# Rounding steps and normalisations written as two-input instructions, and zeros filled elsewhere, in a four-layer sequence kernel

## The chip, the cores and the metric

The kernel runs on one core of one Trainium2 chip. The metric is the device time of one execution in microseconds. Everything is computed in fp32. The engines are TensorE (PE; PEld is its loading of weights), VectorE (DVE), ScalarE (ACT) and GpSimd (POOL); SyncE (SP) issues the DMAs.

## What is computed

The input x has 16 sequences (B) of 512 tokens (T) with 256 channels (C). Four layers run one after the other, each with its input added and a layer normalisation behind it, `(v - mean) / sqrt(var + 1e-5)`:

- attention with 16 heads, causal, whose queries and keys are projected into latents of 32 values and rotated by position;
- a feed-forward layer 256 -> 704 -> 256, `down(silu(gate) * up)`, in which the inputs and weights of the products are first rounded to FP4;
- a recurrence over the 512 tokens with a tanh of its states;
- a channel mix, `sigmoid(xr Wr) * (relu(xk Wk)^2 Wv)`, where xr and xk blend each token with the one before it.

The rounding to FP4 is what the change is about. Each row is cut into blocks of 16 values:

```python
def fp4_quant_dequant(x):
    xb = x.reshape(shape[:-1] + (shape[-1] // BLOCK, BLOCK))
    scale = jnp.max(jnp.abs(xb), axis=-1, keepdims=True) / 6.0
    scale = jnp.maximum(scale, jnp.float32(1e-12))
    xn = xb / scale
    idx = jnp.searchsorted(_MID, jnp.abs(xn))
    q = _GRID[idx] * jnp.sign(xn) * scale
    return q.reshape(shape)
```

## The kernel before

**Stage 1** (about 0 to 1765 us of the profiled execution) runs attention and the feed-forward layer together. A loop (from L788) goes over slots (b, g, n): 16 sequences, 4 groups of heads, 3 pieces of the causal triangle. Each slot computes scores (`S`, L524), masks them and takes their maximum on DVE (L536), takes exponentials on ACT (L549), turns the result on PE (L559; ACT copies it out, L561) and weights the values with it (L590; `vpad` holds the values with zeros between the heads). Beside each half slot the loop places steps of other work by a hand-written plan: latents (PE L457, DVE L467 and L472), values, heads, the output projection of a finished sequence (L482 to L506), and for 128 tokens at a time `quantize`, `ffn_up` (L281 on) and `ffn_down`. The order of PE's instructions is fixed by this program text. The orders of the other engines come from a scheduler, which places instructions by their estimated times.

PE's results go to seven PSUM banks in rotation. A group of matmuls takes the bank used seven groups before and waits until the engine that reads that bank has done so. Two such readers matter below: L304 and L307 in `ffn_up` (DVE, the gate and the product with `up`) and L536.

**The rounding** is `fp4`, L181 to L215, a generator whose `yield`s let the plan spread its instructions: it goes on a list, of which `vector_step` takes one step at a time, and `vector_done` all that a consumer still needs. The DVE part takes the maximum of the block (L201), its scale (L202), the reciprocal (L203), a correction by one unit of the last place (L204), the scaled values (L207), the power of two of each (L209, L210), and adds a constant that rounds (L213). POOL then takes the constant away (L214) and multiplies by the scale (L215). Inputs to `ffn_up` have 256 columns (16 blocks), inputs to `ffn_down` 704 (44 blocks). Their tiles `q_sc`, `q_inv`, `q_q` and `q_m` have two buffers each.

**The normalisations.** The statistics come from DVE (L91, L92), `rstd_of` (L81 to L87) takes the power -0.5 on POOL, and one DVE instruction subtracts the mean and multiplies: L502 behind the attention, L98 in `layernorm` behind the feed-forward layer, L891 in `normalized` in the second half of the kernel.

**Between the stages** (about 1765 to 1860 us) the last output projection is followed by the rounding and the feed-forward layer of the last 512 tokens, in an order given by the list `FIRST` (L1092). `N` in it is `normed`, the first step of the recurrence: DVE L859, POOL L863 to L867, then PE L883. In the same stretch POOL fills `hist`, the buffers of the recurrence's states, with zeros (L1008).

**Stage 2** (from about 1860 us) steps through the 512 tokens (L1167 on): `advance_state` multiplies a state (PE L1060) and takes its tanh on ACT into `hist` (L1068), twice per token, with the other steps of the layers beside it.

At the start of stage 1 DVE copies two columns (`cabk`, L394), while POOL fills `vpad` with zeros (L400). `values` (L415) writes the heads between these zeros later.

Of the kernel before, what the change touches and what calls it, by code (L numbers as in the profile page):

```python
# [10 lines left out]
F32 = mybir.dt.float32  # L11
# [3 lines left out]
AF = mybir.ActivationFunctionType  # L15
ALU = mybir.AluOpType
# [3 lines left out]
P = 128  # L20
B, T, C = 16, 512, 256
# [38 lines left out]
def tile_kernel(ctx: ExitStack, tc: tile.TileContext, I: dict, out: bass.AP):  # L60
    nc = tc.nc


    const = ctx.enter_context(tc.tile_pool(name="const", bufs=1))
# [3 lines left out]
    make_identity(nc, ident)  # L68
    neg_half = const.tile([P, 4], F32, name="neg_half")
    nc.gpsimd.memset(neg_half, -0.5)  # L70
    cols = const.tile([P, NCOLS], F32, name="cols")
    nc.sync.dma_start(cols, I["cols"])

# [7 lines left out]
    def rstd_of(mv, n, eps):  # L81

        ve = small.tile([P, 4], F32, tag="ve", name="ve")
        nc.gpsimd.tensor_scalar(ve[:, :n], mv[:, :n, 1], 1.0, eps, ALU.mult, ALU.add)  # L84
        rs = small.tile([P, 4], F32, tag="rstd", name="rstd")
        nc.gpsimd.tensor_tensor(rs[:, :n], ve[:, :n], neg_half[:, :n], ALU.pow)
        return rs  # L87

    def stats_into(mv_slice, x):
        st = small.tile([P, 6], F32, tag="bnst", name="bnst")  # L90
        nc.vector.bn_stats(st, x)  # L91
        nc.vector.bn_aggr(mv_slice, st)  # L92

    def layernorm(dst, src):
        mv = small.tile([P, 4, 2], F32, tag="mv", name="mv")
        stats_into(mv[:, 0, :], src)
        rs = rstd_of(mv, 1, LN_EPS)
        nc.vector.tensor_scalar(dst, src, mv[:, 0, 0:1], rs[:, 0:1], ALU.subtract, ALU.mult)  # L98

# [3 lines left out]
    def recurrent_weights():  # L105

        ta = own.tile([P, 2, 4, P], F32, name="ta")  # L110
        wb = own.tile([P, 4, 2, 2, P], F32, name="wb")
        nc.gpsimd.memset(wb, 0.0)
        wc = own.tile([P, 4, 2, 32], F32, name="wc")
        nc.gpsimd.memset(wc, 0.0)
        for par, quarters in enumerate(QUARTERS):
            for i, (r, c) in enumerate(quarters):

                e = i % 2
                of, rs, cs = slice(e * 64, e * 64 + 64), slice(r * 64, r * 64 + 64), slice(c * 64, c * 64 + 64)
                nc.sync.dma_start(ta[rs, par, :, cs], I["bda"][of, i // 2 :: 2, of])  # L120
                if par == 0:
                    nc.sync.dma_start(
                        wc[cs, :, r, c * 16 : c * 16 + 16],
                        I["bdc"][of, i // 2 :: 2, e * 16 : e * 16 + 16],
                    )
                for q2 in range(2):
                    at = slice(q2 * 64 + i * 16, q2 * 64 + i * 16 + 16)
                    nc.sync.dma_start(
                        wb[at, q2::2, par, r, cs], I["bdb"][at, q2 * 2 + i // 2 :: 4, of]
                    )  # L130
        nc.scalar.activation(ta, ta, AF.Tanh)
        for k in ("woutT", "wrT", "wkT", "wvT"):
            sq[k] = own.tile([P, 2, C], F32, name=k)
            nc.sync.dma_start(sq[k], I[k].rearrange("(n p) c -> p n c", p=P))
        bout = own.tile([P, C], F32, name="bout")
        nc.sync.dma_start(bout, I["bout"].to_broadcast([P, C]))
        nc.vector.tensor_scalar(bout, bout, 0.5, None, ALU.mult)
        return ta, wb, wc, bout
# [9 lines left out]
    def mm(name):  # L148
        banks.append(banks.pop(0))
        return banks[-1].tile([P, 512], F32, tag="mm", name=name)  # L150
# [30 lines left out]
    def fp4(dst, x, nb, rows=P):  # L181

        n = nb * 16
        sc = ffn.tile([P, 44], F32, tag="q_sc", name="q_sc", bufs=2)[:rows, :nb]  # L190
        inv = ffn.tile([P, 44], F32, tag="q_inv", name="q_inv", bufs=2)[:rows, :nb]
        q = ffn.tile([P, FF], F32, tag="q_q", name="q_q", bufs=2)[:rows, :n]
        m = ffn.tile([P, FF], F32, tag="q_m", name="q_m", bufs=2)[:rows, :n]

        def blocks(t):
            return t.rearrange("p (n k) -> p n k", k=16)

        def over(t):
            return t.unsqueeze(2).to_broadcast([rows, nb, 16])

        nc.vector.tensor_reduce(sc, blocks(x), AX.X, ALU.max, apply_absolute_value=True)  # L201
        nc.vector.tensor_scalar(sc, sc, 1.0 / 6.0, 1e-12, ALU.mult, ALU.max)  # L202
        nc.vector.reciprocal(inv, sc)  # L203
        nc.vector.tensor_scalar(inv, inv, 1.0 - 2.0**-23, None, ALU.mult)  # L204
        if n > C:
            yield
        nc.vector.tensor_tensor(blocks(q), blocks(x), over(inv), ALU.mult)  # L207
        yield
        nc.vector.tensor_scalar(m.bitcast(U32), q.bitcast(U32), 0x7F800000, None, ALU.bitwise_and)  # L209
        nc.vector.tensor_scalar(m, m, 1.0, 1.5 * 2.0**22, ALU.max, ALU.mult)  # L210
        if n > C:
            yield
        nc.vector.tensor_tensor(q, q, m, ALU.add)  # L213
        nc.gpsimd.tensor_tensor(q, q, m, ALU.subtract)  # L214
        nc.gpsimd.tensor_tensor(blocks(dst), blocks(q), over(sc), ALU.mult)  # L215
# [56 lines left out]
    def quantize(b, j):  # L272
        xq_of[b, j] = xq = ffn.tile([P, C], F32, tag="xq", name="xq", bufs=2)
        queue(("x", b, j), fp4(xq, x_of[b][:, j, :], C // 16))
        yield 0.0
# [65 lines left out]
    with ExitStack() as a:  # L341
# [54 lines left out]
            )  # L396

        vpad = [wts.tile([P, NT, H, 32], F32, name=f"vpad{i}") for i in range(2)]
        for i in range(2):
            nc.gpsimd.memset(vpad[i], 0.0)  # L400

# [78 lines left out]
        def out_projection(b):  # L482
            while b not in whole:
                yield None
            x, yT = x_of[b], y_of.pop(b)
            for j in range(0, NT, 2):
                mv = small.tile([P, 4, 2], F32, tag="mv", name="mv")
                ps = mm("ps_o")
                for i in range(2):
                    for hf in range(2):  # L490
                        nc.tensor.matmul(
                            ps[:, i * C : i * C + C],
                            yT[:, hf, (j + i) * P : (j + i) * P + P], cpT[:, hf, :],
                            start=hf == 0, stop=hf == 1,
                        )
                both = x[:, j : j + 2, :].rearrange("p j c -> p (j c)")
                nc.vector.tensor_tensor(both, ps, both, ALU.add)
                for i in range(2):
                    stats_into(mv[:, i, :], x[:, j + i, :])
                rs = rstd_of(mv, 2, LN_EPS)  # L500
                for i in range(2):
                    nc.vector.tensor_scalar(  # L502
                        x[:, j + i, :], x[:, j + i, :], mv[:, i, 0:1], rs[:, i : i + 1],
                        ALU.subtract, ALU.mult,
                    )
                yield 0.9  # L506

# [108 lines left out]
        def pause(b):  # L616
# [9 lines left out]

        TASKS = {
            "L": latents, "H": heads, "V": values, "O": out_projection, "Q": quantize,
            "U": lambda b, j: whole_steps(ffn_up(b, j)), "D": lambda b, j: whole_steps(ffn_down(b, j)),
            "W": lambda b: ffn_weights(), "P": pause,  # L630
# [67 lines left out]
        with tc.manual_schedule(engines={mybir.EngineType.PE}), ExitStack() as s:  # L698
# [8 lines left out]
            rows = prep.tile([1, C], F32, name="rows")  # L707
# [74 lines left out]
        ps_b = five.enter_context(tc.tile_pool(name="ps_b", bufs=5, space=PSUM))  # L782
        ps_y = five.enter_context(tc.tile_pool(name="ps_y", bufs=1, space=PSUM))
        banks[:] = [ps_2] * 2 + [ps_b] * 5

        with tc.manual_schedule(engines={mybir.EngineType.PE}):
            slots = [(b, g, n) for b in range(B) for g in range(4) for n in range(len(BLOCKS))]
# [3 lines left out]
            for slot in slots + [None]:  # L791
                if slot:
                    b, g, n = slot
                    if g == 0 and n == 0:
# [5 lines left out]
                        if b == 2:  # L800
                            ta, wb, wc, bout = recurrent_weights()
# [20 lines left out]
                before = (slot, ps) if slot else None  # L822
            divide()
            last_projection = out_projection(B - 1)
            next(last_projection)
            quantize_now(0)
# [151 lines left out]
    def value(p):  # L978
# [24 lines left out]
    hist = [  # L1003
        [wts.tile([P, 8, 2, 64], F32, name=f"hist{g}{i}") for i in range(2)] for g in range(2)
    ]
    for g in range(2):
        for i in range(2):
            nc.gpsimd.memset(hist[g][i], 0.0)  # L1008
    state = [None, None]
    clean, ot_of = {}, {}  # L1010

# [113 lines left out]
    with tc.manual_schedule(engines={mybir.EngineType.PE}):  # L1125
# [41 lines left out]
        for t in range(T):  # L1167
# [9 lines left out]
            for g in range(2):  # L1177
                if us[g] is None or us[g][0] + us[g][1] == t:
                    t0, n = starts[g].pop(0)
# [6 lines left out]
            if t % 8 == 7:  # L1186
                at = t % 16 - 7
                for g in range(2):
                    old, new = hist[g][t // 8 % 2], clean[t // 16, g]
                    old = old.rearrange("p t k (r s b) -> p t k r s b", r=2, s=2)  # L1190
                    for r in range(2):
                        rs, qs = slice(r * 64, r * 64 + 64), slice(64 - r * 64, 128 - r * 64)
# [108 lines left out]
```

## Time and profile before

| | |
|---|---|
| median of 3 runs | 2583.96 us (2583.03 to 2585.3) |
| profiled execution | 2582.77 us |
| its span, from the first to the last instruction | 2581.0 us |
| mean granted clock of TensorE, as a share of the full | 0.983 |
| instructions in the span | 73861 |

The busy time of the engines in 40 equal slices of the span, in tenths (9 is 90% or more), with the granted clock of TensorE:

```profile
PE   8789999999999999999999999996899999999997
DVE  6767888787887888878888788887566666666665
ACT  4656666666666666666666666753366666666663
POOL 4322333333333333333333333333555555555653
PEclk9899999999999999999999999998899999999999
```

The slice is 64.5 us wide. From the third slice to the 27th the picture hardly changes: that is stage 1. The drop of PE behind it is the stretch between the stages, and the last third is the recurrence. PE is close to full throughout; DVE is the next, at some 80% in stage 1.

The groups of instructions by line give the busy time of a group, the mean time of one instruction in nanoseconds, and after the second bar the idle time of the engine just before it. Those of the rounding's small steps on DVE, separate by form:

```profile
L204 DVE TENSOR_SCALAR q_inv<-q_inv 128x16 f32<-128x16 f32 x74 | 31.2, 424 | 1.0
L202 DVE TENSOR_SCALAR q_sc<-q_sc 128x44 f32<-128x44 f32 x66 | 28.5, 432 | 1.1
L204 DVE TENSOR_SCALAR q_inv<-q_inv 128x44 f32<-128x44 f32 x66 | 23.6, 357 | 1.1
L202 DVE TENSOR_SCALAR q_sc<-q_sc 128x16 f32<-128x16 f32 x74 | 17.9, 253 | 0.2
```

Such a mean can stand far from the usual duration of the instruction, so the views of single lines, with minimum, median and maximum, are read beside it:

```profile
L204 DVE TENSOR_SCALAR q_inv<-q_inv x142: 138/176/1595, 15.5 to 1834.0; 128x16 f32<-128x16 f32 x74, 128x44 f32<-128x44 f32 x66, 64x16 f32<-64x16 f32 x2
L202 DVE TENSOR_SCALAR q_sc<-q_sc x142: 110/186/1470, 14.4 to 1831.8; 128x16 f32<-128x16 f32 x74, 128x44 f32<-128x44 f32 x66, 64x16 f32<-64x16 f32 x2
```

In the timeline, a row is a run of equal instructions on one engine: start and duration in microseconds, what is computed from what, how many, and in square brackets how long the engine had been idle and what ended that. In the view of waits, a row names the waiting engine and line, what it waited for, the total, the number of waits and the longest.

### The profile page before, as it was taken

Reading aid. Unit: us, or ns where it says so; the run is one execution under the profiler, and the core shown is the slowest. Engines: PE = TensorE matmul, PEld = TensorE weight load, DVE = VectorE, ACT = ScalarE, POOL = GpSimd, SP = SyncE. Lnnn points to the kernel's source line nnn. Section 1 sums busy time; section 2 is a strip of 40 time slices with the busy share of each in tenths; the row PEclk is TensorE's granted clock in tenths of the full one; section 3 lists DMA queues with packets and bytes.
Section 4 is the critical chain, followed back from the end, with each engine's and each line's share of the span. In section 5 each row is a group of like instructions: output and inputs, shape, how many; then the busy total and the mean of one; then the engine's idle time right before and its main releaser. Section 6 shows DMA issues by size and latency. Waiting matters only on the chain.

```text
span 2581.0 us, 73861 instructions
## 1 busy us (share of the span) xinstructions
PE 2438.0 (94%) x28802; PEld 1715.8 (66%) x28802; DVE 1946.9 (75%) x5621; ACT 1615.6 (63%) x5532; POOL 1048.2 (41%) x1649
## 2 busy tenths in 40 slices
PE   8789999999999999999999999996899999999997
PEld 4456666666666666666666666664677777777775
DVE  6767888787887888878888788887566666666665
ACT  4656666666666666666666666753366666666663
POOL 4322333333333333333333333333555555555653
PEclk9899999999999999999999999998899999999999
DMA  3000000000000000000000000000101111111100
GB/s 118 22 10 5 22 13 16 13 15 16 19 14 16 15 12 23 14 16 15 12 24 14 15 15 4 15 14 9 49 29 40 37 38 40 40 38 37 35 28 22
DMA packets 58016, 61.30 MB, mean 24 GB/s; under 512 B 7873, under 2 KB 53058, under 8 KB 57666
## 3 DMA queue, kind: packets, MB, share of 16 engines
q1 hardware_dynamic: 56802, 55.54, 6.9%
q8 instruction: 226, 3.70, 0.6%
q10 hardware_dynamic: 864, 1.05, 0.1%
q14 instruction: 124, 1.02, 0.1%
HBM read 39.79 MB, written 16.78 MB: 22 GB/s over the span
## 4 chain that ended last, share of the span: by engine, by line
PE 58%; DVE 27%; ACT 7%; POOL 4%; issue 3%; DMA 0%; ACTq 0%; POOLq 0%; DVEq 0%; SPq 0%
PE u L1060 7%; PE ps_pt L559 6%; PE S L524 5%; DVE p L536 5%; PE u L1020 4%; PE pg L160 4%; PE pu L160 3%; PE py L590 3%; ACT p L549 3%; PE ps_h L439 3%; PE ps_d L160 2%; PE ps_a L904 2%; PE ps_k L904 2%; ACT pT L561 2%; PE ps_q L457 2%
## 5 line engine op out<-in xcount | busy, mean ns | idle before, releaser
L549 ACT ACTIVATE p<-p,nm 128x512 f32<-128x512 f32 (+3 forms) x1024 | 569.7, 561 | 520.8 <-DVE nm L536 516.7
L1068 ACT ACTIVATE hist<-u 64x64 f32<-64x64 f32 x2048 | 447.3, 218 | 250.8 <-PE u L1060 182.5
L536 DVE CUSTOM_DVE_ANT_0 p<-S,mask 128x512 f32<-128x512 f32 (+3 forms) x1024 | 443.7, 483 | 50.1 <-PE S L524 50.1
L559 PEld LDWEIGHTS ps_pt<-ident,p 128*128 128x128 f32 x2560 | 296.7, 141 | 235.5 <-issue 86.2
L1060 PEld LDWEIGHTS u<-hist,ta 128*64 128x64 f32 x8176 | 362.9, 138 | 121.0 <-ACT hist L1068 41.6
L559 PE MATMUL ps_pt<-ident,p 128*128 128x128 f32 x2560 | 393.6, 280 | 9.2 <-DVE nm L536 3.5
L561 ACT COPY pT<-ps_pt 128x384 f32<-128x384 f32 (+1 forms) x768 | 370.3, 515 | 38.9 <-PE ps_pt L559 38.6
L1060 PE MATMUL u<-hist,ta 128*64 128x32 f32 x8176 | 384.2, 219 | 4.8 <-ACT hist L1068 4.5
L214 POOL TENSOR_TENSOR q_q<-q_q,q_m 128x256 f32<-128x256 f32 (+1 forms) x142 | 168.7, 1188 | 457.0 <-DVE q_q L213 442.7
L524 PE MATMUL S<-kc,qr 32*128 32x128 f32 (+3 forms) x2048 | 235.7, 474 | 8.9 <-ACT qr L478 7.9
L1020 PE MATMUL u<-xt,wb 128*64 128x64 f32 x4128 | 223.2, 230 | 3.5 <-issue 2.4
L549 ACT ACTIVATION_READ_ACCUMULATOR p<-p,nm 128x1 f32 x1024 | 198.9, 194 | 0.0
L160 PE MATMUL pg<-wgT,xqT 128*128 128x352 f32 x512 | 177.5, 470 | 4.2 <-ACT xqT L289 2.9
L473 POOL TENSOR_TENSOR qc<-qc,qs 128x512 f32<-128x512 f32 x64 | 81.6, 1275 | 236.0 <-DVE qs L472 230.9
L160 PE MATMUL pu<-wuT,xqT 128*128 128x352 f32 x512 | 172.5, 459 | 1.2 <-DVE th L304 1.2
L160 PE MATMUL ps_d<-wdT,hT 128*128 128x256 f32 x732 | 169.5, 381 | 2.2 <-ACT hT L323 2.2
L1020 PEld LDWEIGHTS u<-xt,wb 128*64 128x64 f32 x4128 | 165.0, 139 | 9.4 <-issue 3.0
L590 PEld LDWEIGHTS py<-pT,vpad 128*32 128x32 f32 x5120 | 141.2, 110 | 43.2 <-issue 30.7
L590 PE MATMUL py<-pT,vpad 128*32 128x128 f32 x5120 | 165.3, 276 | 3.8 <-ACT pT L561 3.5
L524 PEld LDWEIGHTS S<-kc,qr 32*128 32x128 f32 x2048 | 111.0, 185 | 78.2 <-issue 32.0
L160 PEld LDWEIGHTS ps_d<-wdT,hT 128*128 128x128 f32 x732 | 134.8, 191 | 19.6 <-ACT hT L323 3.1
L84 POOL TENSOR_SCALAR ve<-mv 128x1 f32<-128x1 f32 (+1 forms) x160 | 32.8, 205 | 264.5 <-DVE mv L92 234.7
(164 smaller groups left out, 4620.4 us busy)
## 6 DMA issues: line engine op xcount, KB each, us to landing
xT<-in_xT_dram SPq DMA_DIRECT2D x16, 512.0 KB
x<-in_x_dram SPq DMA_DIRECT2D x16, 512.0 KB
xs<-x SPq DMA_DIRECT2D x64, 128.0 KB
x<-xs SPq DMA_DIRECT2D x32, 256.0 KB
xm<-xs SPq DMA_DIRECT2D x32, 256.0 KB
out_dram<-o SPq DMA_DIRECT2D x64, 128.0 KB
w<-in_w_down_dram SPq DMA_DIRECT2D x2, 352.0 KB
w<-in_w_gate_dram SPq DMA_DIRECT2D x5, 128.0 KB
```

Of the source, the lines that this page charges most:

```text
L160: nc.tensor.matmul(dst, left, right, start=start, stop=stop)
L214: nc.gpsimd.tensor_tensor(q, q, m, ALU.subtract)
L524: nc.tensor.matmul(S[h][:, at : at + w], q[rs, i * P : i * P + P], k[rs, :w], start=True, stop=True,)
L536: nc.vector.tensor_tensor_reduce(out=p[:, own], in0=S[h][:, own], in1=mask[:, T - (i + 1) * P :], scale=1.0, scalar=-MASKED, op0=ALU.add, ...
L549: nc.scalar.activation(p[:, own], p[:, own], AF.Exp, bias=nm[:, u : u + 1], scale=-1.0, accum_out=sum_of[b, g][:, cb, half, h : h + 1],)
L559: nc.tensor.transpose(ps[:, at : at + P], p[:, at : at + P], ident)
L561: nc.scalar.copy(pT[:, :w], ps[:, :w])
L590: nc.tensor.matmul(py[q * 32 : q * 32 + 32, PLACE[i][1], :], vpad[b % 2][:, j, g * 4 + h, :], pt, start=j == 0 and h % 2 == 0, stop=j == i ...
L904: nc.tensor.matmul(dst[cs], left[:, cs], right, start=first, stop=not first)
L1020: nc.tensor.matmul(u[rs, k, par:n:2, bs : bs + 16], wb[:, g * 2 + k, par, half, rs], xt[:, g, at : at + n - par : 2, :], start=par == 0 an ...
L1060: nc.tensor.matmul(into[cs, :, c, :], ta[:, t % 2, g * 2 + k, cs], own[:, :, c, :], start=False, stop=True, skip_group_check=True,)
L1068: nc.scalar.activation(state[g][rs, :, r * 32 : r * 32 + 32].rearrange("p k (s b) -> p k s b", s=2), u[rs, :, t - t0, :] .rearrange("p k ( ...
```

## The change

It has four parts.

1. In `fp4` the correction of L204 is no longer an instruction of its own. L207 becomes a SCALAR_TENSOR_TENSOR that multiplies by the constant and by the reciprocal; L202 becomes one too, which takes its lower bound from a small tile `tiny` filled at the start.
2. The normalisations of L98 and L502 change from TENSOR_SCALAR to SCALAR_TENSOR_TENSOR, with the reciprocal deviation spread over the columns as second input. L891 is not changed.
3. The zeros of `vpad` are filled by the same POOL instructions, but written behind the preparation, just ahead of the loop of stage 1.
4. The zeros of `hist` are made by ACT, as the product of another tile (`ta`, weights of the recurrence) with 0, instead of by POOL.

```diff
+    tiny = const.tile([P, 44], F32, name="tiny")
+    nc.gpsimd.memset(tiny, 1e-12)
...
-        nc.vector.tensor_scalar(dst, src, mv[:, 0, 0:1], rs[:, 0:1], ALU.subtract, ALU.mult)
+        nc.vector.scalar_tensor_tensor(
+            dst, src, mv[:, 0, 0:1], rs[:, 0:1].to_broadcast([P, C]), ALU.subtract, ALU.mult
+        )
...
-        nc.vector.tensor_scalar(sc, sc, 1.0 / 6.0, 1e-12, ALU.mult, ALU.max)
+        nc.vector.scalar_tensor_tensor(sc, sc, 1.0 / 6.0, tiny[:rows, :nb], ALU.mult, ALU.max)
         nc.vector.reciprocal(inv, sc)
-        nc.vector.tensor_scalar(inv, inv, 1.0 - 2.0**-23, None, ALU.mult)
         if n > C:
             yield
-        nc.vector.tensor_tensor(blocks(q), blocks(x), over(inv), ALU.mult)
+        nc.vector.scalar_tensor_tensor(
+            blocks(q), blocks(x), 1.0 - 2.0**-23, over(inv), ALU.mult, ALU.mult
+        )
...
         vpad = [wts.tile([P, NT, H, 32], F32, name=f"vpad{i}") for i in range(2)]
-        for i in range(2):
-            nc.gpsimd.memset(vpad[i], 0.0)
...
-                    nc.vector.tensor_scalar(
-                        x[:, j + i, :], x[:, j + i, :], mv[:, i, 0:1], rs[:, i : i + 1],
-                        ALU.subtract, ALU.mult,
+                    nc.vector.scalar_tensor_tensor(
+                        x[:, j + i, :], x[:, j + i, :], mv[:, i, 0:1],
+                        rs[:, i : i + 1].to_broadcast([P, C]), ALU.subtract, ALU.mult,
                     )
...
         banks[:] = [ps_2] * 2 + [ps_b] * 5
+        for i in range(2):
+            nc.gpsimd.memset(vpad[i], 0.0)
...
-            nc.gpsimd.memset(hist[g][i], 0.0)
+            nc.scalar.activation(
+                hist[g][i].rearrange("p t k n -> p (t k n)"), ta.rearrange("p a k n -> p (a k n)"),
+                AF.Identity, scale=0.0,
+            )
```

Line numbers here and below are those of the kernel before, unless another kernel is named.

## Prediction, made before the changed kernel ran

> **What bounds the kernel now.** I read the totals first, then the stage in which nearly all of the rounding runs, then that stage's waits, and last single stretches of its timeline.
>
> ```profile
> PE 2438.0 (94%) x28802; PEld 1715.8 (66%) x28802; DVE 1946.9 (75%) x5621; ACT 1615.6 (63%) x5532; POOL 1048.2 (41%) x1649
> PE 58%; DVE 27%; ACT 7%; POOL 4%; issue 3%; DMA 0%; ACTq 0%; POOLq 0%; DVEq 0%; SPq 0%
> ```
>
> TensorE is busy 94% of the span, yet VectorE, the only engine on which this change removes work, holds 27% of the chain of waits. So DVE time counts only where TensorE waits for it. Stage 1 repeats every 108 us, once per batch, and b = 2 to 14 are 13 such blocks with the same pattern. One block, in the busy times per stretch (PE, PEld, DVE, ACT, POOL, then the granted clock):
>
> ```profile
> 960.00:1068.00 108.00, 106.01 (x850) 70.89 (x849) 89.16 (x267) 71.03 (x212) 37.52 (x45) 1.00 0.05 16
> ```
>
> PE leaves only 2.0 us of 108 idle, at full clock. The waits of stage 1 (200 to 1700 us: total, times, longest) say where they fall, each 13 times, once a block:
>
> ```profile
> PE ps_q L457 <- ACT pT L561: 8.0, 13, 0.7
> PE S L524 <- ACT qr L478: 7.1, 13, 0.5
> PE ps_q L457 <- DVE nm L536: 5.2, 13, 0.4
> PE ps_h L321 <- DVE h L307: 4.4, 13, 0.4
> ```
>
> All are waits for a PSUM bank that another engine has to empty. A wait inside a group of matmuls lengthens the group instead. The change can win perhaps 2 to 3 us a block, or lose more.
>
> **The small steps.** L204, `q_inv` times 1-2^-23, goes: 142 instructions. Median 176 ns, but a sum of 31.2 us (x74) and 23.6 us (x66) by form. One stretch shows why (start, duration):
>
> ```profile
> 1062.33 1.67 POOL L214 TENSOR_TENSOR q_q<-q_q,q_m 128x704 f32<-128x704 f32 x1 [0.90 <-DVE q_q L213]
> 1062.45 1.59 DVE L204 TENSOR_SCALAR q_inv<-q_inv 128x16 f32<-128x16 f32 x1
> 1064.07 0.43 DVE L207 TENSOR_TENSOR q_q<-x,q_inv 128x256 f32<-128x256 f32 x1
> 1064.08 1.67 POOL L215 TENSOR_TENSOR hq<-q_q,q_sc 128x704 f32<-128x704 f32 x1
> 1064.54 1.36 DVE L209 TENSOR_SCALAR q_m<-q_q 128x256 uint32<-128x256 uint32 x1
> 1066.31 2.52 PE L524 MATMUL S<-kc,qr 32*128 32x384 f32 x8
> ```
>
> The 16-column L204 ends 40 ns behind POOL's L214, and L209 0.15 us behind L215: DVE is held up by POOL. The blocked L204 do not simply vanish: the next instruction, L207, takes their place. Where do they go? By the trace, L213, with two SBUF inputs, was held up in 8 of 8 cases under a POOL TENSOR_TENSOR, but L207, with two as well, in 1 of 14 under a POOL COPY. So the waits under L214 and L215 move to L207, while L202, in its new form, escapes L575's copies (13 cases, one a block, some 0.2 us each): 2.6 us of DVE. The Trainium skill ("SBUF — State Buffer", SBUF: two separate sides) has a DVE instruction with two SBUF inputs wait for any GpSimd instruction that reads SBUF, a copy too: then 0. Either way L204 itself saves the plain 142 x about 0.13 = 18 us of DVE, and none of this is time until PE is seen to wait.
>
> Here L207 would end at L214's end, 1064.00, plus 256 elements at 0.96 per ns: 1064.27 at the latest, for 1064.50. L215 and L209 follow it, with 0.1 us more from the L204 of the 704-wide rounding ahead. L304 and L307 then free banks earlier, and the S group, 2.52 us where the same eight take 0.93 to 1.03 elsewhere in the block, gets them: **-0.4 us a block**. Bounds: 0 (if L215 keeps its start, L209 still waits for it) and -1.5 (the whole of 2.52 over 1.03).
>
> L202 and L207 change form with two SBUF sources and an immediate. Nearest rows: L207 itself, a TENSOR_TENSOR with the same two inputs, 891 ns at 704 columns, and L304, an SCALAR_TENSOR_TENSOR of 352 columns in 518 = 352/0.96 + 151. By both L207 keeps its time. L202's two-input form may cost 0 to 30 ns more, hidden in L204's removal.
>
> **Where a rule speaks against it.** The Trainium skill ("Vector Engine (DVE) Microarchitecture Reference", Points that are easy to get wrong) says that a scalar_tensor_tensor with two non-bf16 SBUF sources runs at half throughput. The rows, minimum/median/maximum:
>
> ```profile
> L207 DVE TENSOR_TENSOR q_q<-h,q_inv x64: 849/891/1010, 179.9 to 1834.8; 128x704 f32<-128x704 f32 x64
> L502 DVE TENSOR_SCALAR x<-x,mv,rstd x64: 394/414/3670, 153.1 to 1787.9; 128x256 f32<-128x256 f32 x64
> L942 DVE SCALAR_TENSOR_TENSOR mur<-d,cols,x3T x64: 471/480/618, 1877.6 to 2565.4; 128x256 f32<-128x256 f32 x64
> L991 DVE SCALAR_TENSOR_TENSOR x<-th,x x32: 683/890/892, 1910.5 to 2573.1; 128x512 f32<-128x512 f32 x32
> ```
>
> L991 has two fp32 SBUF sources, and its minimum is 512/0.96 + 150; halved it would be 1217, over its maximum. I go by the rows. By the rule L207 would take 2 x 704/0.96 + 150 = 1617, so +0.73 us x 66, +0.26 x 76 at 256 columns, and +0.34 x 128 normalisations: +111 us of DVE.
>
> **The normalisations** L98 and L502 (64 each) get L942's form, two sources and a pointer: 480 for 414, +0.07 us each, 8.4 us of DVE in all (bounds 0 and the rule's 0.34). L891, in the recurrence, stays. PE never waits for L98, whose result goes to a store. But DVE's next instructions stand behind it; at two of the block's four places these release PSUM, so **+0.1 us a block**.
>
> **What moves.** A comparison of both programs' instruction lists shows PE unchanged, SP with one pair of DMAs swapped, and these shifts in each block:
>
> ```profile
> 1031.24 1.50 DVE L502 TENSOR_SCALAR x<-x,mv,rstd 128x256 f32<-128x256 f32 x2 [0.87 <-POOL rstd L86]
> 1088.05 0.51 DVE L307 SCALAR_TENSOR_TENSOR h<-th,pu 128x352 f32<-128x352 f32 x1
> 1088.48 0.88 DVE L213 TENSOR_TENSOR q_q<-q_q,q_m 128x704 f32<-128x704 f32 x1
> 1088.61 0.88 PE L321 MATMUL ps_h<-ident,hq 128*128 128x128 f32 x6 [0.37 <-DVE h L307]
> ```
>
> In the first row two normalisations take 1.50 instead of 2 x 0.41, because L214 and L215 of a 256-wide rounding run beside them. In the new order L213, which starts those two, comes after the next L536. So -0.68, +0.13 for their form, -0.1 for L204; the L536 behind them free the banks of L559, ps_q and ps_k: **-0.65 a block** (bounds -0.8 and 0).
>
> At 1088 the new order puts L210 and the 704-wide L213 ahead of L307, for which PE waits already. L307 comes 0.88 later less the 0.18 of L204: +0.70 for PE there. The three L536 that stood behind it now stand ahead and come 0.46 earlier, up to the ps_q wait at 1098.8, which idled PE for 0.65. I take the pair at **-0.25** (bounds: +0.70 if nothing is given back, -0.35).
>
> Sum: -0.65 - 0.4 - 0.25 + 0.1 = -1.2 us a block, x 13 = **-15.6 us**. The first two and the last batch, with other neighbours, I take at 0 (+-2).
>
> **Zeros of the states.** Between the stages:
>
> ```profile
> 1780.55 3.62 POOL L1008 MEMSET hist<- 128x1024 f32 x4
> 1780.64 3.98 DVE L502 TENSOR_SCALAR x<-x,mv,rstd 128x256 f32<-128x256 f32 x2 [0.44 <-POOL rstd L86]
> 1836.11 1.14 PE L883 MATMUL ps_xn<-ident,xn 128*128 128x128 f32 x4 [1.78 <-POOL xn L867]
> ```
>
> The memsets hold L502 up by 3.98 - 0.8 = 3.2 us. On ACT four activations of 1024 columns, some 2 x 561 (L549 at 512) = 1.1 us each, 4.5 in all, lie in the 14.73 us for which ACT idles before L289's copy at 1790.41; without that cover they would cost 4.5. But the new order also sets L502, which waits for rstd, ahead of L209, L210 and L213 of the first rounding, so PE's ps_xq keeps only some 2.0 us, and later 704-wide roundings move ahead of the steps L859 to L867, with L214 and L215 (2 x 1.67) ahead of L863 to L867 on POOL, for which PE already waits 1.78 at 1836. I take the whole transition at **+1.4** (bounds -3, the hold-up saved, and +4).
>
> **Zeros of the padded values.** At the start:
>
> ```profile
> 3.19 6.05 DVE L394 COPY cabk<-cols 64x2 f32<-64x2 f32 x2
> ```
>
> It is held up by the memsets, two of 1.8 us (3.36 to 6.91) foremost. The new place in the source puts them behind one memset of 0.2 us only; they wait for nothing and run as early: 0. That part doesn't do what it says. Bounds 0 and -3. The recurrence (1860 on) keeps its order on DVE and ACT: 0.
>
> **Sum.** 2582.77 - 15.6 + 1.4 = 2568.6 for the profiled execution (span 2581.0, 1.8 outside it). The median before is 1.2 above that execution: 2569.8, so **2570**. Own range 2560 to 2579, by -1.9 to -0.5 a block and the transition's ends.
>
> **Rivals.**
> - *More is won* (0.10). L204 stood on the chain for 29.6 us of 200 to 1700 (my sum over the chain); if all of it went, with 3 for the memsets and 2.8 given back by normalisations (a third of 8.4, DVE's share there): 2554. Against it: the waits move to L207, and PE has 2 us a block to give.
> - *Nothing* (0.13). PE, 106 of 108, absorbs what DVE gains: 2583. For it: ACT releases head two of the four waits.
> - *Slower: L307 queued behind the wide L213* (0.18). At 1088 PE loses 0.70 in each block, 13 x 0.70 = +9.1; it decides if L536's earlier end only moves the wait to ACT's pT (8.0 us of waits already) and the gains at 1031 and 1066 stay under 0.5 us together (13 x (0.8 - 0.5) + 1.4 = 5.3). With none of them, and with the transition's 1.4 and 1.3 of L98: 2596.
> - *Half throughput* (0.04). Of +111 us DVE a third, its chain share there, on the path, with gains of none: +37 to +45, some 2625.
>
> **Numbers.** Own 0.55. A measurement can tell +-0.2%, 5.2 us. Faster: 0.52 of my case and the first rival, 0.62; same: 0.03 and most of the second, 0.15; slower 0.23. The range 2550 to 2597 holds all but the last rival and tails.
>
> **What would show it.** L204 gone, L207 at 704 columns still near 0.89, at 256 columns with a maximum near 1.6 (the wait has moved). L98 and L502 near 0.48, L502's maximum far under 3.67. The wait of ps_h for L307 well over 4.4; that of ps_q for L536 under 5.2. The copy cabk still near 6 us. I am wrong if stage 1 keeps its 108 us blocks, or L207 nears 1.6 at its minimum.

## The result, and the profile after

The changed kernel takes 2572.55 us in the median of 6 runs (2569.47 to 2575.44), the kernel before 2583.3 in the runs beside them: ratio 0.9957, with a 95% interval of 0.9947 to 0.9968. It is faster by 10.7 us; 2570 was forecast. Its profiled execution took 2574.87 us with a span of 2573.1, so 7.9 us less than the profiled one before.

The line numbers of the changed kernel are a little higher: L202 is L206 now, L207 is L210, L209 is L214, L213 to L215 are L218 to L220, L307 is L312, L331 is L336, L457 is L460, L467 is L470, L502 is L505, L98 is L100, L883 is L888.

First the busy times on the page of the changed kernel:

```profile
PE 2440.3 (95%) x28802; PEld 1724.2 (67%) x28802; DVE 1925.5 (75%) x5479; ACT 1618.4 (63%) x5536; POOL 1042.3 (41%) x1646
```

DVE has 142 instructions and 21.4 us less, and the time fell by half of that. Then the views of the changed lines (minimum/median/maximum in ns):

```profile
L210 DVE SCALAR_TENSOR_TENSOR q_q<-x,q_inv x64: 359/422/1573, 164.3 to 1786.1; 128x256 f32<-128x256 f32 x64
L210 DVE SCALAR_TENSOR_TENSOR q_q<-h,q_inv x64: 876/891/1882, 181.7 to 1817.7; 128x704 f32<-128x704 f32 x64
L505 DVE SCALAR_TENSOR_TENSOR x<-x,mv,rstd x64: 474/482/487, 155.1 to 1769.8; 128x256 f32<-128x256 f32 x64
```

The medians of the rounding are what they were (891 at 704 columns), and nothing runs at half rate. The maxima are new: 1573 ns at 256 columns. That is L204's wait for POOL, at its new place. The stretch that the prediction quoted now reads, in the timeline of the changed kernel:

```profile
1053.34 0.96 POOL L578 COPY rcx<-rc 128x256 f32<-128x256 f32 x1 [12.66 <-DVE rc L576]
1053.95 0.37 DVE L206 SCALAR_TENSOR_TENSOR q_sc<-q_sc,tiny 128x16 f32<-128x16 f32 x1
...
1054.26 1.68 POOL L219 TENSOR_TENSOR q_q<-q_q,q_m 128x704 f32<-128x704 f32 x1
...
1054.64 1.57 DVE L210 SCALAR_TENSOR_TENSOR q_q<-x,q_inv 128x256 f32<-128x256 f32 x1
1056.01 1.45 POOL L220 TENSOR_TENSOR hq<-q_q,q_sc 128x704 f32<-128x704 f32 x1
1056.25 1.36 DVE L214 TENSOR_SCALAR q_m<-q_q 128x256 uint32<-128x256 uint32 x1
```

L210 starts while POOL's L219 runs and ends 0.27 us behind it; in the kernel before, L207 ended 0.50 us behind L214. So the wait has moved, and against POOL some 0.23 us are saved here. L206 still takes 0.37 us under POOL's copy, as L202 did at this place.

By form, over the whole span: L204's 55.7 us are gone; L207 rose from 85.7 to 112.5 us as L210 (x64 each at 704 and 256 columns, without the weights); L202 fell from 46.4 to 38.4; L209 rose from 71.3 to 75.2; L502 fell from 36.8 to 28.2; L98 rose from 26.4 to 31.0. Nearly half of what L204 had cost came back at L207.

Three waits of TensorE in stage 1 (200 to 1700 us) of the changed kernel: the one that was feared, and two that the rows of before did not show:

```profile
PE ps_h L326 <- DVE h L312: 3.6, 8, 0.7
PEld ps_ks L460 <- DVE x L336: 2.9, 13, 0.2
PEld ps_ks L460 <- DVE kc L470: 2.8, 13, 0.2
```

The two waits of ps_q that the prediction's rows show, 8.0 us for ACT's pT and 5.2 for L536, are in no row of the changed kernel any more: 13.2 us of waits that are gone.

Where the time went is best seen through TensorE. Both kernels have the same PE instructions in the same order, 28802 records each; so the n-th record of one is paired with the n-th of the other, and the difference of their start times is taken. Some records can be missing, so a few tenths are not meaningful. Each column is a single execution, and that moves by more: e3, whose only edit acts at 1780 us, is 1.5 us ahead at 200 us already. In us, at the times of the kernel before (minus is earlier; the columns e1 to e10 are the experiments below):

```
before    after     e1      e5      e6      e7      e10
  200      1.7     1.6     1.9     2.1     0.4      3.1
  312      4.9     2.6     4.7     3.4    -0.2      6.6
  960     -6.3   -11.6    -7.3    -8.9   -13.8      5.6
 1700    -18.0   -25.9   -21.2   -21.3   -29.4      4.6
 1765    -15.0   -24.6   -18.2   -18.3   -28.1      6.3
 1790    -17.0   -24.5   -18.0   -20.1   -30.4      4.1
 1830    -16.3   -23.4   -16.4   -19.4   -30.0      5.4
 1837    -10.4   -17.6   -10.6   -13.6   -24.2     12.6
 2500     -9.1   -17.2    -9.7   -12.1   -23.3     12.2
```

From 312 to 1700 us, 12.9 blocks, 23.0 us are won. 4.9 us are lost ahead of that, and 7.6 between 1700 and 1837. From there to the end 2.5 are added.

### The profile page after: what moved, and what is told of

The parts are those of the page before. It is cut to its first block, busy times and chain, and to the rows that moved or that the text cites. A ratio compares the mean times of both kernels' runs of the same rounds, so it can differ in the third digit from the quotient of the medians.

```text
span 2573.1 us, 73749 instructions
## 1 busy us (share of the span) xinstructions
PE 2440.3 (95%) x28802; PEld 1724.2 (67%) x28802; DVE 1925.5 (75%) x5479; ACT 1618.4 (63%) x5536; POOL 1042.3 (41%) x1646
## 4 chain that ended last, share of the span: by engine, by line
PE 58%; DVE 25%; ACT 9%; issue 3%; POOL 3%; DMA 0%; ACTq 0%; DVEq 0%; POOLq 0%
PE u L1069 7%; PE ps_pt L562 6%; PE S L527 5%; DVE p L539 5%; PE u L1029 4%; ACT p L552 4%; PE ps_d L164 4%; PE py L593 4%; ACT pT L564 3%; DVE q_q L210 3%; PE pg L164 2%; PE pu L164 2%; PE ps_a L909 2%; PE ps_h L442 2%; PE ps_k L909 2%
## 5 line engine op out<-in xcount | busy, mean ns | idle before, releaser
L539 DVE CUSTOM_DVE_ANT_0 p<-S,mask 128x512 f32<-128x512 f32 (+3 forms) x1024 | 442.9, 484 | 51.4 <-PE S L527 51.4
L219 POOL TENSOR_TENSOR q_q<-q_q,q_m 128x256 f32<-128x256 f32 (+1 forms) x142 | 166.7, 1174 | 418.9 <-DVE q_q L218 416.9
```

Source lines behind the costliest of these rows:

```text
L539: nc.vector.tensor_tensor_reduce(out=p[:, own], in0=S[h][:, own], in1=mask[:, T - (i + 1) * P :], scale=1.0, scalar=-MASKED, op0=ALU.add, ...
```

## The experiments

All ratios are to the kernel before, run on the same chip in the same stretch of time.

**One part at a time.** e1 has the rounding's edits alone, e2 the normalisations, e3 the zeros of the states, e4 those of the padded values. The diffs are the four parts shown above.

> Only the rounding of the change (L202 and L207 as two-input instructions, L204 gone). If the gain of stage 1 is the rounding's, as the prediction has it, this kernel has all of it: PE reaches 1690 us of the kernel before some 16 to 20 us earlier, and the whole is 9 to 17 us under the kernel before (about 0.994 to 0.9965), with ps_q waiting less for L536 and ps_h as long as after the change. If instead the normalisations or the zeros carried it, it is within 3 us of the kernel before. If the loss of some 6 us between the stages (PE L883) comes from the rounding's new order, it is seen here too.

Measured: 2565.56 us against 2582.96, ratio 0.9935 (0.9923 to 0.9948). The rounding alone wins 17.4 us by the medians, more than the whole change, though the two intervals just touch; its column shows the loss of 5.8 us at 1830 to 1837 too. The gain is the rounding's, and so is that loss.

> Only the normalisations L98 and L502 as two-input instructions. By the prediction they cost 0.07 us each and 0.1 us a block on the path: +1 to +3 us (ratio 1.000 to 1.0015), medians of L98 and L502 near 482 ns. If they helped because a two-input instruction escapes more of POOL's work, -3 us or more. By the rule of half throughput the medians would be near 750 ns and the time +10 or more.

Measured: 2585.39, ratio 1.0005 (0.9998 to 1.0012). Alone the normalisations cost 1.3 us by the ratio and 2.4 by the medians, as forecast, and can't be told from no change.

> Only the zeros of the states by ACT. L502 between the stages falls from 3.67 to 0.41 us at most, and PE's ps_xq (1789.7) comes 2 to 3 us earlier. If that gain is kept to the end: -2 to -3 us. If PE's wait for POOL's L867 at 1836 takes it back, as the prediction thought: within 1 us of the kernel before.

Measured: 2580.49, ratio 0.9991 (0.9985 to 0.9998), so 2.5 us by the medians, with an interval from 0.5 to 3.9. L502's maximum is 805 ns, for 3670, and PE's ps_xq comes 2.2 us earlier. The prediction had this lost again. The trace can't tell: against the lead of 1.6 us that e3 has at 1765 us, it is 2.2 us ahead at 1790, 0.5 at 1837 and 1.4 at 2500. The medians speak for a part that is kept.

ACT is not needed to end this hold-up. In e2 and e6 POOL still fills the states, and L502 in its new form is not held up by it. In e6, where L505 is L502, L204 is L202 and L212 is L209:

```profile
1762.21 3.61 POOL L1011 MEMSET hist<- 128x1024 f32 x4
1762.30 0.88 DVE L505 SCALAR_TENSOR_TENSOR x<-x,mv,rstd 128x256 f32<-128x256 f32 x2 [0.43 <-POOL rstd L88]
1763.76 0.16 DVE L204 SCALAR_TENSOR_TENSOR q_sc<-q_sc,tiny 128x16 f32<-128x16 f32 x1
1764.90 1.07 DVE L212 TENSOR_SCALAR q_m<-q_q 128x256 uint32<-128x256 uint32 x1
```

Under the memsets two normalisations take 0.88 us, for 3.98 as TENSOR_SCALAR; L212, still a TENSOR_SCALAR, is held up to their end. PE's ps_xq comes 1.8 us earlier, for 2.0 in the changed kernel. In e2 the next small step is still a TENSOR_SCALAR: it takes the wait over (2.09 us at 1782.36), and 0.7 us are won. So parts 1 and 2 of the change remove most of what part 4 removes; the change with POOL's zeros was not run.

> Only the zeros of the padded values moved in the program. By the prediction nothing moves on the chip: the memsets still run at 3.5 to 7 us, the copy cabk still takes near 6 us, and the time is within 1 us. If the move does what its place suggests, cabk takes under 0.3 us and the time falls by up to 3 us.

Measured: 2582.08, ratio 0.9998 (0.9989 to 1.0006). The time is as forecast, the reason is not. In e4 DVE's copy is free:

```profile
3.06 0.35 DVE L394 COPY cabk<-cols 64x2 f32<-64x2 f32 x2
9.31 0.23 DVE L374 TENSOR_SCALAR w<-w 128x128 f32<-128x128 f32 x1 [5.91 <-DMA w<-in_bdw_dram]
```

The two copies take 0.35 us for 6.05, but the next instruction waits for the transfer of `in_bdw` and starts at 9.31, where it started at 9.28 before. The transfer covers the copy. In the changed kernel the copy is again held up (6.05 us from 3.44): there `cols` landed 0.4 us later, and POOL had begun its memsets. The memsets themselves moved by 0.4 us only.

**Why the whole wins less than one of its parts.** The sum of the four parts is -17.4 + 2.4 - 2.5 - 0.9 = -18.4 us, the whole -10.7. e5 and e6 add one normalisation each to the rounding, e7 is the change without both:

```diff
 e5: rounding, and  L98 -> scalar_tensor_tensor
 e6: rounding, and L502 -> scalar_tensor_tensor
 e7: rounding, zeros of the states and of the padded values; L98 and L502 as before
```

> The rounding's edits and L98 as a two-input instruction; L502 as before. The rounding alone took 17.4 us off, the whole change 10.7. If the 7 us between them come from L98's 0.07 us in front of bank releases: about 2572 (ratio near 0.996). If they come from L502: within 2 us of the rounding alone, 2565 to 2568, with the 64 matmuls of ps_ks not waiting for the residual sum of L331.

> The rounding's edits and L502 as a two-input instruction; L98 as before. If L502 is what costs: its 2 x 0.07 us set the sum of L331 behind the start of ps_qs, so that ps_ks starts one pass of 0.51 us late in 12 blocks: +6 us on the rounding alone, 2570 to 2573. If L98 is: within 2 us of the rounding alone.

> The change without its normalisations. By sums of the parts: the rounding's -17.4, with -2.5 of the states' zeros and nothing of the padded values: 2563 (ratio 0.9925). If the 7 us were the zeros' fault when beside the new rounding, it stays near 2572.

Measured: e5 2569.97, ratio 0.9947 (0.9934 to 0.9959); e6 2568.8, ratio 0.9943 (0.9929 to 0.9957); e7 2560.82, ratio 0.9916 (0.9903 to 0.993). Both times lie between the two cases that each expectation named. The intervals of e1, e5 and e6 overlap, so the times don't tell these three apart; e7 is clear of the whole change, so the normalisations together do cost something beside the new rounding. The rest is read from the traces. From 312 to 1700 us e5 loses 2.5 us on e1, some 0.2 a block, and e6 3.7 us, some 0.3 a block; the whole change loses 5.4.

In e6 the forecast mechanism is seen. First e1's timeline, where the bank (of PSUM) for ps_ks is free before it is wanted:

```profile
917.01 0.41 DVE L334 TENSOR_TENSOR x<-ps_d,x 128x256 f32<-128x256 f32 x1
...
917.52 0.69 PE L460 MATMUL ps_qs<-heads,bdqs 64*128 64x512 f32 x1
...
917.53 0.69 PE L460 MATMUL ps_ks<-heads,bdks 64*128 64x512 f32 x1
```

Then the same place in e6:

```profile
919.67 0.42 DVE L334 TENSOR_TENSOR x<-ps_d,x 128x256 f32<-128x256 f32 x1
...
920.14 0.29 PEld L460 LDWEIGHTS ps_ks<-heads,bdks 64*128 64x128 f32 x2 [0.22 <-DVE x L334]
920.14 0.69 PE L460 MATMUL ps_ks<-heads,bdks 64*128 64x512 f32 x1
```

In e1 ps_qs and ps_ks, which use 64 rows each of TensorE, start 10 ns apart and run side by side. In e6 ps_qs starts at 919.62, while L334, the residual sum that empties the bank for ps_ks, ends at 920.09. ps_ks starts 0.52 us behind: the wait that the view shows is 0.2 us, but that the two no longer run side by side costs PE 0.51. When the two traces are compared, PE had been 0.2 us better just ahead, since in e6 the first L536 comes ahead of the rounding's L213 (L539 and L216 in e6) and not behind it, so that 0.3 a block is left. So the length is not all: from the start of L502 (L505 in e6) to that of L334 DVE takes 4.40 us in e1 and 4.68 in e6, and the two longer normalisations are 0.15 of these 0.28. The row of this wait is there 13 times in e6 (2.9 us) and not at all in e1; the changed kernel has it too. So has e2 (13 times, 4.6 us), where ps_ks starts 0.65 us behind ps_qs. There PE is 0.7 us better just ahead, since ps_q's wait for L536 is gone, and from 312 to 1700 us e2 loses nothing.

L98 has a similar place. In e5, and in the changed kernel, ps_ks waits 13 times for `kc` (L470 there), which DVE computes behind L98. But this pair of products is apart in e1 already, by 0.43 us (875.80 and 876.23), and in e5 by 0.51 (879.85 and 880.36). Here 0.07 us on DVE cost 0.08 on PE, near the 0.1 forecast for L98: one us in 13 blocks. The other 1.5 of e5's 2.5 us were not located. The order of DVE's instructions is not their cause, since from 312 to 1700 us it is the same in e1 and e5; but e7 and e8, which don't differ there at all, come out 1.2 us apart in these blocks.

By the medians the step from e7 to the whole change is 2572.55 - 2560.82 = 11.7 us, by the ratios (0.9957 - 0.9916) 10.6. In the traces it is 11.3 at 1700, of which 6.2 arise in the blocks from 312 on, and 5.2 before. Of those 5.2, 3.3 lie between 240 and 260 us, where the granted clock differs: in the five microseconds from 245 and from 250 it is 0.58 and 0.73 in the changed kernel, 0.60 and 0.72 in e5, 0.66 and 1.00 in e1 and e6, and 1.00 twice in e7, e9 and the kernel before. Why some have this drop and others don't was not found: e2, with the normalisations alone, has none, and e10, which has neither of them, has it (0.69 and 0.63, below). With one profile for each kernel it may belong to the execution. So about half of what the normalisations cost in the whole change arises in the blocks, where waits at bank releases behind them are seen. Most of the rest sits in a stretch with a lowered clock, and whether it is theirs is open.

**Is it the form or the absence of L204?**

> The change without its normalisations, and with L202 as a TENSOR_SCALAR as before: of the rounding only L204 goes and L207 takes over its factor. If L202's two-input form buys nothing (in the changed kernel it still takes 368 ns under POOL's copy, as before): within 2 us of the kernel without normalisations, 2559 to 2563. If that form spares DVE waits under POOL: +3 us or more on it.

> The change without its normalisations, but L204 stays as an instruction that multiplies by 1.0, with L202 and L207 in their new form. DVE's order in stage 1 is then nearly that of the kernel before. If the gain comes from L204's leaving and the order that follows: near the kernel before less the zeros, 2578 to 2583. If the new forms of L202 and L207 carry it: 2562 to 2568.

The edits against e7:

```diff
 e9
-        nc.vector.scalar_tensor_tensor(sc, sc, 1.0 / 6.0, tiny[:rows, :nb], ALU.mult, ALU.max)
+        nc.vector.tensor_scalar(sc, sc, 1.0 / 6.0, 1e-12, ALU.mult, ALU.max)
 e10
         nc.vector.reciprocal(inv, sc)
+        nc.vector.tensor_scalar(inv, inv, 1.0, None, ALU.mult)
```

Measured: e9 2561.77, ratio 0.992 (0.9907 to 0.9933), as e7: the edit of L202 is worth nothing that can be told. e10 2593.64, ratio 1.0039 (1.0024 to 1.0053). From 312 to 1700 e10 wins 2.0 us, 0.15 a block, where e7 wins 29.1: with L204 in place, the new forms bring nearly nothing, and DVE's order in the blocks is that of the kernel before. That instruction, by form at 16 columns, takes again what it took, 31.5 us for 31.2. Of DVE's 3298 other instructions from 312 to 1700 us only 12 stand elsewhere than in the kernel before (154 in e1), and both waits of ps_q are back (200 to 1700 us):

```profile
PE ps_q L459 <- ACT pT L563: 8.2, 13, 0.9
PE ps_q L459 <- DVE nm L538: 5.2, 13, 0.4
```

So the gain is L204's leaving, together with the order that the scheduler makes without it. These two were not separated: no kernel was run that had the new order with L204's cost, or the old order without it. That e10 is 11 us slower than the kernel before was not expected. Its column places it: 6.6 us by 312, of which 3.1 fall on the lowered clock near 250, and 7.2 between 1830 and 1837, outside the blocks.

**The stretch between the stages.** e8 is e7 with the squares of the recurrence's first three steps (L859) at high priority:

```diff
-        for i in range(2):
-            nc.vector.tensor_tensor_reduce(
+        for i in range(2):
+            with tc.high_priority() if p < 3 else ExitStack():
+                nc.vector.tensor_tensor_reduce(
...
```

> The change without its normalisations, and with L859 of the first three steps of the recurrence ahead of the rounding of the last tokens on DVE. In the changed kernel PE's L883 comes 3.9 and 2.2 us later than the rest of the gain (at 1832 and 1836 of the kernel before). If DVE's place for L859 does that: 4 to 6 us under the kernel without normalisations, some 2558. If the cost only moves to the down products, which wait for the rounding now put behind: within 2 us of it.

Measured: 2558.57, ratio 0.9905 (0.9891 to 0.9918), the fastest of all, but its interval overlaps that of e7. The two waits of PE for POOL's `xn` (4.68 and 3.69 us idle ahead of L886 in e7) are gone, as the first case had it. But ps_h now waits 1.6 us for DVE's `xt`, and the inputs `u` (L1027 in e7, L1028 in e8) start after 4.25 us of idle time instead of 1.82, so some 4 of these 8.4 us come back. From 1790 to 1837 us e8 loses 0.9 us where e7 loses 6.2: DVE's place for L859 was the cause of that loss. In the times little of this is seen. At 1790 us e8's execution is 3.9 us behind e7's, 2.3 of them from stage 1 and before, though the order of DVE's instructions is the same in both up to there: so much two executions differ. At 1837 e8 is 1.4 us ahead, and 2.3 by the medians.

## Why the prediction was right, and where it wasn't

The forecast of 2570 is 2.6 us from the measured 2572.55. But it is right as a sum, with terms that erred both ways; that they nearly cancelled is luck. In us:

| term | forecast | in the traces |
|---|---|---|
| 13 blocks of stage 1 | -15.6 | -23.0 (312 to 1700 us) |
| start and first batches | 0 (+-2) | +4.9 at 312 |
| between the stages | +1.4 | +7.1 (1700 to 1850) |
| recurrence | 0 | +3.0 (1850 on) |
| profiled executions | -14.2 | -7.9 |

The profiled execution of the changed kernel was one of its slower ones: the medians differ by 10.7. The 3.0 us of the recurrence were not explained. With the same instructions there, e1 and e5 lose nothing (-0.6 and -0.7), e6 and e7 2.8 and 2.9.

*L204's wait moves to L207.* Right: L204's waits, 55.7 - 142 x 0.176 = 31 us (the prediction put the plain instruction at 0.13), became 27 at L207, with a maximum of 1573 ns where "near 1.6" stood. That the blocked instruction is replaced by its successor, and only the plain cost is won, is the step that kept the forecast from the 2554 of the rival.

*Under POOL's copies L202 escapes.* Wrong. All 13 of the L206 that met L578's copy were held up, 0.37 us as before. The Trainium skill's statement in "SBUF — State Buffer", which the prediction set aside for L207's 1 in 14, is what the trace shows for this instruction. The kernel before shows it for L207 too, and the 1 in 14 was misread. These were the instructions at 256 columns, and all but that one had begun before the copy. At 704 columns the copy began first, and L207 was held up in 13 of 13 cases (1007 to 1010 ns, for 891), as here:

```profile
876.38 0.40 POOL L575 COPY rcx<-rc 128x256 f32<-128x256 f32 x1
876.51 1.01 DVE L207 TENSOR_TENSOR q_q<-h,q_inv 128x704 f32<-128x704 f32 x1
```

The step had no weight in the sum, and e9 shows none.

*Half throughput.* L210's minimum is 876 ns at 704 columns where the rule made 1617: the rows were the better guide. L98 and L502 have medians of 485 and 482, as L942 had promised.

*The four terms of a block.* One block (1068 to 1176 us) can be followed in the paired traces. At the release of S (1067 and 1175) -0.42 for the forecast -0.4. At 1088 PE's ps_h loses 0.48, forecast +0.70, and over the stretch to 1101 it comes out at -0.92 where -0.25 stood: this is the term that was mis-sized most, because DVE's earlier L536 gave back 1.40, nearly three times what L307 had cost, 0.75 of it at the ps_q wait of 1098.8. In the stretch at 1031 (1141 in this block) -0.3 for -0.65; the late start of ps_ks took half a microsecond of it. And -0.51 at 1077 to 1082, where L307 again frees a bank of S earlier, was not foreseen. What the rival "slower" named, L307 behind the wide L213, happened, but the wait of ps_h came 8 times with 3.6 us in all, for 13 times with 4.4 before. It was paid back.

*The normalisations.* The prediction had 0.1 us a block for L98 and 0.13 in L502's stretch, 3.0 in all. L98's was right in size at the one place that was found (0.08), while e5 loses 0.2 a block in all. L502's was not: some 0.3 a block is left of a loss of 0.51. In the traces two 64-row products ran side by side only where both banks were free in time, and the step read the cost of a delay from the length of the delay. In the blocks both came to 6.2 us, twice the forecast.

*The zeros of the states.* The hold-up of 3.2 us went, as it would have by the new form of L502 alone (e6). ACT's four instructions of 1.04 us lie in its idle time:

```profile
1764.64 3.90 ACT L1014 ACTIVATE hist<-ta 128x1024 f32<-128x1024 f32 x4 [3.88 <-PE ps_o L494]
1765.72 0.88 DVE L505 SCALAR_TENSOR_TENSOR x<-x,mv,rstd 128x256 f32<-128x256 f32 x2 [0.43 <-POOL rstd L88]
```

ACT's next work, the copy of ps_xq at 1773.44, waits for PE another 4.90 us. PE's ps_xq came 2.0 us earlier, as the prediction had it, though e6 wins 1.8 of them without ACT's zeros. The delay of the steps L859 to L867 was foreseen in kind and mis-sized: it is 5.8 us at PE's L883 (1830 to 1837), where the whole transition had been netted to +1.4 with an upper end of +4. e1 has the same 5.8, so it belongs to the rounding's order. Another 3.0 us are lost from 1700 to 1765, where the granted clock in the changed kernel is 0.66 from 1740 to 1745; before it is 1.00 there. e1 and e7, at 1.00 as well, lose 1.3 of these 3.0.

*The start.* The +4.9 were not foreseen. 3.2 of them fall between 200 and 312 us, with the lowered clock told above; in e7, without it, PE wins 0.6 us in this stretch. The 1.7 us at 200 are no more than single executions differ by there. What set the clock down was not tested.

## What to carry to other kernels

An instruction that is long only because it waits for another engine does not save its duration when it is removed: look which instruction comes next there and whether it waits for the same. A small cost on an engine with little slack can't be multiplied by its share of the path: find the release that it delays, and what TensorE loses if that release comes just too late. And when a scheduler orders the other engines, removing an instruction changes more than that instruction: compare the orders, and look at the stretches outside the steady state, where the new order was not as lucky.

## What the runs showed of the hardware

- Two products on 64 rows each ran side by side when both could start (7 to 10 ns apart), and the second started 0.51 us behind the first when its bank came late; the row of the wait shows 0.2 us of it.
- A SCALAR_TENSOR_TENSOR on DVE with two fp32 inputs in SBUF took 422 ns at 256 columns and 891 at 704 with an immediate, as the TENSOR_TENSOR that it replaced (418 and 891); with a pointer it took 482 at 256, some 60 ns more.
- A DVE instruction with two inputs in SBUF was held up by a COPY of POOL that had begun first (13 of 13 of L206 after, 13 of 13 of L207 at 704 columns before), as by its TENSOR_TENSOR. By POOL's MEMSET it was not (0.88 us for two L505 in e6), while a TENSOR_SCALAR and a COPY of DVE were (3.98 and 6.05 us).
- TensorE's granted clock fell for some microseconds at a time: in all kernels between the stages, and in some near 250 us (0.50 from 246 to 252 in the changed kernel), with full clock for over 1000 us behind. Where it fell near 250 the changed kernel lost about 3 us, as much as its runs spread to either side of their median.
